# A six-layer decoder on one core: the first cross layer's keys, statistics and query rows in space of their own, and single buffers in the first softmax

## The chip, the core and the metric

The kernel runs on one core of a Trainium2 chip. The core has five engines that each run their own queue of instructions in order and meet through semaphores: TensorE (PE, matrix products), VectorE (DVE), ScalarE (ACT), GpSimd (POOL) and SyncE (SP), which here only issues DMAs. The metric is the time of one execution on the device in microseconds; lower is better.

## What is computed

The reference is a decoder of six sublayers over `x` of shape (64, 128, 256) (64 batches of 128 positions, 256 features), all in float32. Each sublayer normalises its input and adds its result to `x`:

```python
x = x + _L0_attn_ref(_layernorm(x), ...)                      # A: attention in a window of 7
x = x + _L0_xattn_ref(_layernorm(x), ctx, ctx, mask, Wp, bp)  # B: masked attention over ctx
x = x + _L0_ffn_ref(_layernorm(x), ...)                       # C: slots
x = x + _L1_attn_ref(_layernorm(x), ...)                      # D: causal attention with a learned bias
x = x + _L1_xattn_ref(_layernorm(x), ctx, ...)                # E: attention over ctx
x = x + _L1_ffn_ref(_layernorm(x), ...)                       # F: quantised weights, convolution
```

Two of them matter here. The first layer, A, softmaxes the scores of each query against 7 neighbouring keys and weighs them with a learned profile `conn` before it normalises again:

```python
attn = softmax(einsum('bhld,bhlwd->bhlw', Q, Kw) / sqrt(DH))
fw = attn * conn
fw = fw / (fw.sum(axis=-1, keepdims=True) + 1e-09)
out = einsum('bhlw,bhlwd->bhld', fw, Vw)
```

The first cross layer, B, has no projections of queries, keys and values: its queries are the normalised rows of `x`, its keys and values the rows of `ctx`, in 16 heads of 16. A score whose query or key is masked is replaced by -1e9, and the weights are multiplied by that mask again.

## The kernel before

**Groups and stages.** The 64 batches are cut into 16 groups of four (`GB`). The layers run one after the other in stages: `stage_window` (A), `stage_cross0` (B, with the slot layer C run inside it by `tick`), `stage_attn` twice (D and E) and `stage_bitnet` (F). Between stages `x` goes through DRAM: `Flow` (L62) loads a group by one DMA of 512 KB on SP's queue (L80, into one of eight buffers) and stores a finished group (L90).

**Layer A.** The generator `window_project` does a group's layer norm statistics and its q, k and v. `ln_stats` (L122) issues per group four pairs `bn_stats`, `bn_aggr` (L141, L142) and an addition (L143) on DVE, and a power (L144) on POOL that gives one over the standard deviation. `row_bias` (L262) is the small DVE operation behind it. The projections are L166 on PE. `window_products` (L320) multiplies shifted keys and queries on POOL, `window_scores` (L332) sums them on PE. `window_softmax` is called once a group: the maximum L348, the difference L350, the exponential on ACT L351, the product with `conn` L353, two sums L356 and L357, the combined sum L358, a reciprocal L359, and the weights `fw` L361. It takes its tiles `m`, `e`, `ec`, `se`, `scn`, `fw` from the pool `wa`, which holds two buffers for each. `window_values` spreads `fw` over the positions on PE (L372), multiplies it with the shifted values into `pv` (L378) and sums to `oT` (L382) on DVE; `window_out` multiplies by the output weights (L175, PE) and adds to `x` (L392, DVE). In its loop the stage staggers these steps over several groups. At the last step of a group, from the second on, it also runs one entry of the list `later`, which prepares a later layer: `prep_b` (for B), `prep_c`, `prep_f`, `prep_d`, and then six steps of `prep_fire`, which builds the bias table of D.

**Layer B's preparation.** `prep_cross0` (L752) loads the output weights, their bias and the mask, builds in `head_rows` the small masks `par`, `row` and `one`, and writes the mask rows (0 or -1e9) to the DRAM tile `mrow`.

**Layer B itself.** `stage_cross0` (L652) begins by filling two key buffers `kt0` and `kt1` (128x4x512, float32, 8 KB in each partition) with the columns of `one`: four copies each on POOL (L661). Four value tiles `va` are cleared and given a column of ones (L665, L666), the first context group is loaded (L645) and the first `x` group. `load_keys(0)` then issues 16 DMAs on SP for the keys of group 0: eight of 64 KB from `ctxT` (L679) and eight mask rows from `mrow` (L680). `prep(bi)` is called per batch. On the first batch of a group it loads the next group, calls `ln_stats`, makes `r4` (L695) and the row bias `nm` (L262). For every batch ACT makes the query rows `qp` (L704) and fills `va` (L708). `more` transposes `qp` on PE (L717) and writes the queries `qt` on ACT (L721). `attention_stage` (L579) clears two `negmax` tiles on POOL, and runs two half steps per batch: PE scores in bursts (L490), a maximum on DVE (L517), its transposition into the queries (L529, L531), the shifted scores and their exponential on ACT (L513), the weighing of the values (L543), the division (L555) and the output.

**What sets the order.** Each engine's queue is written out when the program is built. The tile framework places an instruction in its engine's queue where its operands and its buffer allow, which can be ahead of instructions that stand earlier in the Python text, and it sets the semaphores. A tile in a pool can't be written before the earlier user of the same space has finished, so where a pool is opened decides how early its first instruction can stand. In the kernel before, the pools of `stage_cross0` (`wb`, `wb1`, `wb3`, `wc2`) are opened after those of `stage_window` (`wa`, `wa1`) are closed, and lie on the same space. DMAs of SP go out in the order of its queue. The functions of the change, as they stand before:

Of the kernel before, what the change touches and what calls it, by code (L numbers as in the profile page):

```python
# [16 lines left out]
D = 256  # L17
H = 16
DH = 16
S = 128  # L20
# [319 lines left out]
def window_softmax(k, w, t, wp, w1):  # L340
    nc = k.nc
    sv = t.scp[:, 0 : WIN * 64].rearrange("p (w l) -> p l w", l=64)

    def over(x):
        return x.unsqueeze(2).to_broadcast([128, 64, WIN])

    m = wp.tile([128, 64], F, tag="m", name="m")
    nc.vector.tensor_reduce(m, sv, AX.X, ALU.max)  # L348
    e = wp.tile([128, 64, WIN], F, tag="e", name="e")
    nc.vector.tensor_tensor(e, sv, over(m), ALU.subtract)  # L350
    nc.scalar.activation(e, e, AF.Exp)  # L351
    ec = wp.tile([128, 64, WIN], F, tag="ec", name="ec")
    nc.vector.tensor_tensor(ec, e, w.conn.unsqueeze(1).to_broadcast([128, 64, WIN]), ALU.mult)  # L353
    se = wp.tile([128, 64], F, tag="se", name="se")
    sc = wp.tile([128, 64], F, tag="scn", name="scn")
    nc.vector.tensor_reduce(se, e, AX.X, ALU.add)  # L356
    nc.vector.tensor_reduce(sc, ec, AX.X, ALU.add)  # L357
    nc.vector.scalar_tensor_tensor(se, se, 1e-9, sc, ALU.mult, ALU.add)  # L358
    nc.vector.reciprocal(se, se)  # L359
    t.fw = wp.tile([128, 64, WIN], F, tag="fw", name="fw")  # L360
    nc.vector.tensor_tensor(t.fw, ec, over(se), ALU.mult)  # L361
# [289 lines left out]
def stage_cross0(k, w, wc):  # L651
# [3 lines left out]
    with k.tc.tile_pool(name="wb", bufs=2) as wp, k.tc.tile_pool(name="wb1", bufs=1) as w1, \  # L655
            k.tc.tile_pool(name="wb3", bufs=3) as w3, k.tc.tile_pool(name="wc2", bufs=2) as c2:
        kts, vas = [], []
        for i in range(2):
            kt = w1.tile([128, 4, GB * S], F, name=f"kt{i}")
            for c in range(4):  # L660
                nc.gpsimd.tensor_copy(kt[:, c], w.one[:, c : c + 1].to_broadcast([128, GB * S]))  # L661
            kts.append(kt)
        for i in range(4):
# [7 lines left out]

        def load_keys(g):


            kt = kts[g % 2]
            for par in range(2):
                for r in range(4):
                    rows = slice(32 * r + 16 * par, 32 * r + 16 * par + 16)
                    nc.sync.dma_start(out=kt[rows, par::2, :], in_=k.a["ctxT"][g, rows])  # L679
                    nc.sync.dma_start(  # L680
                        out=kt[32 * r + 20 - 16 * par : 32 * r + 21 - 16 * par, par::2, :],
                        in_=w.mrow[g : g + 1].unsqueeze(1).to_broadcast([1, 2, GB * S]),
                    )

        load_keys(0)

        def prep(bi):
            g, b = divmod(bi, GB)
            if b == 0:
                k.flow.reach(g + 1)  # L690
                if g + 1 < k.G:
                    cxs[g + 1] = load_group(k, wp, g + 1, 3)
                mv, rs = ln_stats(k, wp, g)
                r4 = wp.tile([S, GB], F, tag="r4", name="r4")
                nc.vector.tensor_scalar(r4, rs, 0.25, None, ALU.mult)  # L695
                stats[g] = r4, row_bias(k, wp, mv, r4)
            r4, nm = stats[g]
# [4 lines left out]
            xb = k.x[g][:, b, :]  # L702
            qp = wp.tile([S, D], F, tag="qp", name="qp")
            nc.scalar.activation(  # L704
# [46 lines left out]

def prep_cross0(k, pool):  # L752
    nc = k.nc
    w = Ctx()
    w.wp = load(k, pool, "b_wp")
    w.bp = load_row(k, pool, "b_bp")
    w.mask = load(k, pool, "mask")
    w.mask2 = pool.tile([S, k.NB], F, name="mask2")
    nc.vector.tensor_tensor(w.mask2, w.mask, w.mask, ALU.mult)
    w.par = pool.tile([128, 2], F, name="b_par")  # L760
    w.row = pool.tile([128, 2], F, name="b_row")
    w.one = pool.tile([128, 4], F, name="b_one")
    head_rows(k, w.par, w.row, w.one)

    w.mrow = k.dram.tile([k.G, GB * S], F, name="mrow")
    with k.tc.tile_pool(name="maskw", bufs=1) as cp:
        mr = load(k, cp, "maskr")
        nc.vector.tensor_scalar(mr, mr, 0.0, -1.0e9, ALU.is_equal, ALU.mult)
        nc.sync.dma_start(out=w.mrow, in_=mr)
    return w  # L770

# [286 lines left out]
def prep_fire(k, pool):  # L1058
# [4 lines left out]
    with k.tc.tile_pool(name="firew", bufs=1) as cp:  # L1063
# [21 lines left out]

        bm = cp.tile([S, 4, 4, S], F, name="bm")
        nc.scalar.copy(bm, b2.rearrange("p (c r) -> p r c", r=4).unsqueeze(3).to_broadcast([S, 4, 4, S]))
        bmf = bm.rearrange("p r c l -> p (r c) l")
        nc.gpsimd.affine_select(bmf, bmf, [[0, 16], [1, S]], ALU.is_ge, NEG, 0, -1)
        yield  # L1090
# [13 lines left out]
        for half in range(2):  # L1104
# [8 lines left out]
            for q in range(2):  # L1113
                pv = ps[:, q].rearrange("p (t c r) -> p r c t", c=4, r=4)
                own = slice(64 * half + 32 * q, 64 * half + 32 * q + 32)
                for r in range(4):
                    nc.vector.tensor_tensor(bt[:, r, :, own], pv[:, r], bm[:, r, :, own], ALU.add)
            yield
# [384 lines left out]
def decoder(tc, a):  # L1503
# [8 lines left out]
    with ExitStack() as ctx:  # L1512
# [10 lines left out]
        with tc.tile_pool(name="w1", bufs=1) as w1:  # L1523
            with tc.tile_pool(name="w0", bufs=1) as w0:
                with tc.tile_pool(name="wA", bufs=1) as wA:
# [3 lines left out]
                    def prep_b():  # L1529
                        p.b = prep_cross0(k, w0)  # L1530

# [142 lines left out]
```

## Time and profile before

| | |
|---|---|
| time, median of 3 runs | 3145.78 us (3145.59 to 3149.34) |
| time of the profiled execution | 3156.87 us |
| its span in the trace | 3155.1 us |
| mean granted clock of TensorE | 0.92 |
| busy: PE, of it weight loads beside | 2773.7 us (88%), PEld 1784.5 us (57%) |
| busy: DVE | 2343.6 us (74%) |
| busy: ACT | 1600.3 us (51%) |
| busy: POOL | 453.4 us (14%) |
| layer A ends (last L392) | 570.3 us |
| layer B's first maximum (L517) begins | 586.73 us |

Every time within the kernel is counted from the start of the span of one profiled execution. The engines' busy times overlap, so they don't add up to the span. A row of the timeline has the start, the busy time of the group, the engine and line, the operation with its output and inputs, the number of instructions, and in brackets how long the engine had been idle and what released it. The row "L490 ... sm<-kt,qt" is thus the score matmul of line 490 with output `sm`. The profile's page counts for the whole span 256 maxima L517 of 1221 ns, 128 products L320 of 1995 ns and 64 powers L144 of 1059 ns into `ln_rs`, the form that A, B and some later stages share.

### The profile page before, as it was taken

How to read it: one execution, taken by the hardware profiler on the slowest of the kernel's cores; microseconds unless marked ns; L12 is line 12 of the kernel's file. 1: busy time of each engine (PE TensorE's matmuls, PEld its weight loads, DVE VectorE, ACT ScalarE, POOL GpSimd, SP SyncE). 2: the span in 40 equal slices, each digit the busy share in tenths (PEclk: the TensorE clock that was granted, in tenths of full speed). 3: DMA queues.
4: the chain of work that ended last, by engine and by line, in shares of the span. 5: the costliest groups of instructions: out<-in, count | busy, mean ns of one | idle time of the engine just before them, and what ended most of it. 6: DMA issues, size and time to landing. Idle time of an engine off the chain costs nothing.

```text
span 3155.1 us, 63533 instructions
## 1 busy us (share of the span) xinstructions
PE 2773.7 (88%) x26850; PEld 1784.5 (57%) x26876; DVE 2343.6 (74%) x4533; ACT 1600.3 (51%) x2684; POOL 453.4 (14%) x358
## 2 busy tenths in 40 slices
PE   5889988689989899889999999979999998888887
PEld 2334533466666677546666666656666665334343
DVE  7898788757777777568888888845455546898897
ACT  3132221366656566445555555455555556766663
POOL 7565663100000000010000000020000000100000
PEclk9888888789999899889999999989999999999898
DMA  4110101201111111100000000011111101011000
GB/s 152 42 39 29 41 27 40 76 29 38 53 56 42 46 32 35 41 29 15 28 28 28 28 28 28 28 48 42 42 54 48 42 29 41 14 40 34 27 21 27
DMA packets 60012, 123.83 MB, mean 39 GB/s; under 512 B 9088, under 2 KB 34064, under 8 KB 59472
## 3 DMA queue, kind: packets, MB, share of 16 engines
q1 hardware_dynamic: 59168, 118.28, 10.9%
q8 instruction: 213, 3.49, 0.4%
q0 software_dynamic: 560, 1.49, 0.2%
q14 instruction: 71, 0.58, 0.1%
HBM read 77.76 MB, written 41.98 MB: 38 GB/s over the span
## 4 chain that ended last, share of the span: by engine, by line
PE 50%; DVE 35%; ACT 8%; POOL 3%; DMA 2%; issue 2%; SPq 0%; POOLq 0%; DVEq 0%; ACTq 0%
PE ps L175 9%; PE ps L166 8%; PE sm L490 8%; PE ps L543 4%; PE se L490 4%; DVE negmax L517 3%; PE ps L1189 3%; PE cv L1370 3%; DVE sb L504 3%; DVE e L510 3%; DVE hs L1424 2%; DVE pv L378 2%; DVE hp L1360 2%; DVE oT L382 2%; PE ps L555 2%
## 5 line engine op out<-in xcount | busy, mean ns | idle before, releaser
L490 PE MATMUL sm<-kt,qt 32*128 32x128 f32 x6144 | 537.0, 297 | 68.1 <-DVE negmax L517 39.7
L490 PEld LDWEIGHTS sm<-kt,qt 32*128 32x128 f32 x6144 | 434.8, 192 | 239.4 <-DVE negmax L517 72.3
L490 PE MATMUL se<-q,kt 32*128 32x128 f32 x6144 | 481.0, 292 | 55.3 <-DVE e L510 26.2
L517 DVE TENSOR_REDUCE negmax<-sm 128x8 f32<-128x1024 f32 x256 | 312.6, 1221 | 238.2 <-PE se L490 232.0
L490 PEld LDWEIGHTS se<-q,kt 32*128 32x128 f32 x6144 | 402.5, 193 | 82.8 <-issue 36.9
L513 ACT ACTIVATE e<-se 128x1024 f32<-128x1024 f32 x256 | 261.4, 1021 | 168.1 <-PE se L490 160.1
L1370 PE MATMUL cv<-hp,taps 128*128 128x512 f32 x480 | 247.9, 654 | 35.6 <-DVE hp L1360 35.3
L320 POOL TENSOR_TENSOR pr<-pad,qt 128x896 f32<-128x896 f32 x128 | 252.5, 1995 | 168.3 <-PE s L332 128.3
L548 ACT COPY avs<-ps 128x512 f32<-128x512 f32 x192 | 112.2, 584 | 192.1 <-PE ps L543 192.1
L504 DVE TENSOR_TENSOR sb<-sm,bias_s 128x1024 f32<-128x1024 f32 x128 | 156.0, 1219 | 63.4 <-PE se L490 60.2
L511 ACT ACTIVATE e<-e 128x1024 f32<-128x1024 f32 x128 | 135.3, 1057 | 123.6 <-DVE e L510 123.3
L1370 PEld LDWEIGHTS cv<-hp,taps 128*128 128x128 f32 x480 | 95.5, 209 | 143.8 <-issue 86.5
L378 DVE TENSOR_TENSOR pv<-sc,pad 128x896 f32<-128x896 f32 x128 | 139.1, 1093 | 43.7 <-PE sc L372 43.7
L144 POOL TENSOR_TENSOR ln<-ln,expo 128x4 f32<-128x4 f32 x32 | 32.3, 1008 | 960.7 <-DVE ln L143 708.6
L144 POOL TENSOR_TENSOR ln_rs<-ln_ve,expo 128x4 f32<-128x4 f32 x64 | 67.7, 1059 | 652.3 <-DVE ln_ve L143 451.9
L510 DVE TENSOR_TENSOR e<-se,bias_t 128x1024 f32<-128x1024 f32 x128 | 155.6, 1215 | 2.4 <-ACT e L511 1.3
L517 DVE TENSOR_REDUCE negmax<-sb 128x8 f32<-128x1024 f32 x128 | 154.8, 1209 | 0.0
L382 DVE TENSOR_REDUCE oT<-pv 128x128 f32<-128x896 f32 x128 | 139.2, 1093 | 1.2
L372 PE MATMUL sc<-fw,spread 32*128 32x448 f32 x512 | 105.3, 664 | 33.6 <-DVE pv L378 28.9
L531 DVE TENSOR_TENSOR q<-ps,qt 128x512 f32<-128x512 f32 x192 | 130.9, 682 | 1.6 <-PE ps L529 1.6
L555 PE MATMUL ps<-ident,avs 128*128 128x128 f32 x768 | 119.2, 279 | 0.8 <-ACT avs L548 0.8
L141 DVE BATCH_NORM_STATS2 ln_st<-x 128x6 f32<-128x256 f32 x256 | 99.3, 426 | 10.6 <-DMA x<-ab 9.4
(338 smaller groups left out, 5819.9 us busy)
## 6 DMA issues: line engine op xcount, KB each, us to landing
x<-in_x_dram SPq DMA_DIRECT2D x16, 512.0 KB
ab<-x SPq DMA_DIRECT2D x16, 512.0 KB
x<-ab SPq DMA_DIRECT2D x16, 512.0 KB
cx<-in_ctx_dram SPq DMA_DIRECT2D x16, 512.0 KB
kt<-in_ctxT_dram SPq DMA_DIRECT2D x128, 64.0 KB
cd<-x SPq DMA_DIRECT2D x16, 512.0 KB
x<-cd SPq DMA_DIRECT2D x16, 512.0 KB
de<-x SPq DMA_DIRECT2D x16, 512.0 KB
```

The costliest lines, as they stand in the source:

```text
L166: k.nc.tensor.matmul(out, w[:, kc, c0 : c0 + cn], rhsT[:, kc, n0 : n0 + n], start=(kc == 0), stop=(kc == 1),)
L175: k.nc.tensor.matmul(out, aT[:, kc, :], w[:, kc, :], start=(kc == 0), stop=(kc == 1))
L320: k.nc.gpsimd.tensor_tensor(pr[:, c], shift_windows(t.kt, b, c), t.qt[:, c, b, :].unsqueeze(1).to_broadcast([128, WIN, S]), ALU.mult,)
L378: nc.vector.tensor_tensor(pv, bc[th][:, :, 0 : WIN * 64].rearrange("p c (l w) -> p c l w", w=WIN), shift_windows2(t.vt, b, th), ALU.mult,)
L382: nc.vector.tensor_reduce(oT[:, :, 64 * th : 64 * th + 64], pv, AX.X, ALU.add)
L490: k.nc.tensor.matmul(ts[side][:, rr, c * S : (c + 1) * S], st[rows, c, :], mv[rows, c, :], start=True, stop=True,)
L504: nc.vector.tensor_tensor(sb, src, bias_s[:, hf * 2 : hf * 2 + 2, :], ALU.add)
L510: nc.vector.tensor_tensor(e, est, bias_t[:, hf * 2 : hf * 2 + 2, :], ALU.add)
L513: nc.scalar.activation(e, est, AF.Exp)
L517: nc.vector.tensor_reduce(b.lay.extra(b.nm, hf * 2), src.rearrange("p r (c m) -> p r c m", m=S), AX.X, ALU.max, negate=True,)
L555: nc.tensor.transpose(tv[:, c * S : (c + 1) * S], b.avs[:, c, :], k.ident)
L1370: nc.tensor.matmul(pc, w.taps[:, CONV_PE.index(j), t, :], hp[:, :, t : t + S], start=(t == 0), stop=(t == 2),)
```

## The change

Three things are moved, and the arithmetic stays the same.

1. In `window_softmax` all tiles but `fw` come from the pool `wa1`, which has one buffer for each instead of two.
2. A new pool `wbe` with two buffers is opened around `stage_window` and `stage_cross0`, beside `w0`. The statistics tiles, `r4`, `nm` and the query rows `qp` of layer B come from it. `kt0` comes from `w0` now, so neither lies on space of the window stage. Filling `kt0`, and `load_keys(0)`, with its 16 DMAs, are called at the end of `prep_cross0`, that is in the window stage's loop; `kt1` is still filled at the head of `stage_cross0`.
3. `prep_fire` has no temporary `bm` any more: the causal part of the bias table is written straight into `bias_t` and added to in place.

```diff
 def window_softmax(k, w, t, wp, w1):
-    m = wp.tile([128, 64], F, tag="m", name="m")
+    m = w1.tile([128, 64], F, tag="m", name="m")
...
-    e = wp.tile([128, 64, WIN], F, tag="e", name="e")
+    e = w1.tile([128, 64, WIN], F, tag="e", name="e")
...
-    ec = wp.tile([128, 64, WIN], F, tag="ec", name="ec")
+    ec = w1.tile([128, 64, WIN], F, tag="ec", name="ec")
...
-    se = wp.tile([128, 64], F, tag="se", name="se")
-    sc = wp.tile([128, 64], F, tag="scn", name="scn")
+    se = w1.tile([128, 64], F, tag="se", name="se")
+    sc = w1.tile([128, 64], F, tag="scn", name="scn")
...
 def stage_cross0(k, w, wc):
-        kts, vas = [], []
-        for i in range(2):
-            kt = w1.tile([128, 4, GB * S], F, name=f"kt{i}")
-            for c in range(4):
-                nc.gpsimd.tensor_copy(kt[:, c], w.one[:, c : c + 1].to_broadcast([128, GB * S]))
-            kts.append(kt)
+        kts, vas, early, load_keys = w.kts, w.vas, w.early, w.load_keys
+        w.make_keys(w1)
...
-        load_keys(0)
-
         def prep(bi):
...
-                mv, rs = ln_stats(k, wp, g)
-                r4 = wp.tile([S, GB], F, tag="r4", name="r4")
+                mv, rs = ln_stats(k, early, g)
+                r4 = early.tile([S, GB], F, tag="r4", name="r4")
                 nc.vector.tensor_scalar(r4, rs, 0.25, None, ALU.mult)
-                stats[g] = r4, row_bias(k, wp, mv, r4)
+                stats[g] = r4, row_bias(k, early, mv, r4)
...
-            qp = wp.tile([S, D], F, tag="qp", name="qp")
+            qp = early.tile([S, D], F, tag="qp", name="qp")
...
-def prep_cross0(k, pool):
+def prep_cross0(k, pool, early):
...
+    w.kts, w.vas = [], []
+
+    def make_keys(pool):
+        kt = pool.tile([128, 4, GB * S], F, name=f"kt{len(w.kts)}")
+        for c in range(4):
+            nc.gpsimd.tensor_copy(kt[:, c], w.one[:, c : c + 1].to_broadcast([128, GB * S]))
+        w.kts.append(kt)
+
+    w.make_keys = make_keys
+    make_keys(pool)
...
+    load_keys(0)
     return w
...
-        bm = cp.tile([S, 4, 4, S], F, name="bm")
-        nc.scalar.copy(bm, b2.rearrange("p (c r) -> p r c", r=4).unsqueeze(3).to_broadcast([S, 4, 4, S]))
-        bmf = bm.rearrange("p r c l -> p (r c) l")
-        nc.gpsimd.affine_select(bmf, bmf, [[0, 16], [1, S]], ALU.is_ge, NEG, 0, -1)
+        nc.scalar.copy(bt, b2.rearrange("p (c r) -> p r c", r=4).unsqueeze(3).to_broadcast([S, 4, 4, S]))
+        btf = bt.rearrange("p r c l -> p (r c) l")
+        nc.gpsimd.affine_select(btf, btf, [[0, 16], [1, S]], ALU.is_ge, NEG, 0, -1)
...
-                    nc.vector.tensor_tensor(bt[:, r, :, own], pv[:, r], bm[:, r, :, own], ALU.add)
+                    nc.vector.tensor_tensor(bt[:, r, :, own], pv[:, r], bt[:, r, :, own], ALU.add)
...
-            with tc.tile_pool(name="w0", bufs=1) as w0:
+            with tc.tile_pool(name="w0", bufs=1) as w0, tc.tile_pool(name="wbe", bufs=2) as wbe:
...
-                        p.b = prep_cross0(k, w0)
+                        p.b = prep_cross0(k, w0, wbe)
```

The body of `load_keys` moves along unchanged.

Set side by side, the two kernels' queues read as follows. PE's order is the same. On SP the store of `mrow` and the 16 loads of `kt0` now stand ahead of the load of `x` of group 4. On POOL four of the eight key copies stand near the start, and the powers L144 of the cross layer's groups 0 to 3 stand in the window stage. On DVE the statistics of the cross layer's groups 0 to 3 stand there too; the statistics of the window stage's groups 5 to 7 and some small rows of D, E and C (`bqs`, `bks`, `bvb`, `c_hs`) have moved from ahead of the first softmax to behind it. On ACT the first two query rows `qp` stand in the window stage. Behind the hand-over from A to B nothing differs.

More of the change, by code (lines that the diff above doesn't have):

```diff
@@ L670, in stage_cross0 @@
         stats = {}
[L672 to L683, printed above, removed]
-        load_keys(0)
         def prep(bi):
@@ L749, in head_rows @@
         k.nc.vector.tensor_reduce(one[:, c : c + 1], rows[:, 1 - c % 2, c], AX.X, ALU.add)
-def prep_cross0(k, pool):
+def prep_cross0(k, pool, early):
     nc = k.nc
     w = Ctx()
+    w.early = early
     w.wp = load(k, pool, "b_wp")
@@ L769, in prep_cross0, with load_keys @@
         nc.sync.dma_start(out=w.mrow, in_=mr)
+    w.kts, w.vas = [], []
[6 more added lines that the diff above has]
+    make_keys(pool)
+    def load_keys(g):
+        kt = w.kts[g % 2]
+        for par in range(2):
+            for r in range(4):
+                rows = slice(32 * r + 16 * par, 32 * r + 16 * par + 16)
+                nc.sync.dma_start(out=kt[rows, par::2, :], in_=k.a["ctxT"][g, rows])
+                nc.sync.dma_start(
+                    out=kt[32 * r + 20 - 16 * par : 32 * r + 21 - 16 * par, par::2, :],
+                    in_=w.mrow[g : g + 1].unsqueeze(1).to_broadcast([1, 2, GB * S]),
+                )
+    w.load_keys = load_keys
+    load_keys(0)
     return w
```

## The prediction

> **What bounds the kernel now.** I read the profile's page first: its chain that ended last is half TensorE (PE 50%) and a third VectorE (DVE 35%), and the change touches only the first 600 of 3155 us: the first layer (to 570 us), its start and the hand-over to the first cross layer. The table of 20 us windows shows no engine full there (0 to 600 us: PE 498, DVE 494, ACT 146, POOL 338 us busy), so engines wait for one another, and what counts is which wait ends last. The chain of waits and the timelines show it in three places.
>
> The hand-over, in the timeline of all engines:
>
> ```profile
> 569.93 0.42 DVE L392 TENSOR_TENSOR x<-ps,x 128x256 f32<-128x256 f32 x1 [1.84 <-PE ps L175]
> 570.04 4.50 POOL L661 COPY kt<-b_one 128x512 f32<-128x512 f32 x8 [3.91 <-PE ps L175]
> ...
> 576.87 2.00 POOL L144 TENSOR_TENSOR ln_rs<-ln_ve,expo 128x4 f32<-128x4 f32 x2
> ...
> 579.50 1.09 ACT L704 ACTIVATE qp<-x,ln_nm,r 128x256 f32<-128x256 f32 x2 [2.47 <-DVE ln_nm L262]
> ...
> 581.54 2.19 PE L490 MATMUL sm<-kt,qt 32*128 32x128 f32 x16 [0.21 <-issue]
> ...
> 586.73 1.21 DVE L517 TENSOR_REDUCE negmax<-sm 128x8 f32<-128x1024 f32 x1
> ...
> 588.00 2.15 PE L490 MATMUL sm<-kt,qt 32*128 32x128 f32 x16 [4.27 <-DVE negmax L517]
> ```
>
> The first layer ends at 570.3; then a serial chain runs: 8 key copies, 8 memsets and the power L144 on POOL, statistics, query rows, scores. The first maximum waits 3 us more, because DVE still does statistics of other groups. It ends at 587.9.
>
> The steady first layer: one softmax (L348) per group of four batches cuts it into blocks. Starts 235.34, 262.17, 289.06 give 26.8 and 26.9 us; starts 393.90, 424.20, 454.71, 485.32, 513.63, 539.18 give 30.3, 30.5, 30.6, 28.3, 25.6. The slow ones hold no layer norm statistics (L141); the quick ones do. DVE, then PE, first a quick block, then a slow one:
>
> ```profile
> 268.26 0.22 DVE L358 SCALAR_TENSOR_TENSOR se<-se,scn 128x64 f32<-128x64 f32 x1
> 271.79 1.98 DVE L361 TENSOR_TENSOR fw<-ec,se 128x448 f32<-128x448 f32 x1
> ...
> 429.03 1.46 DVE L358 SCALAR_TENSOR_TENSOR se<-se,scn 128x64 f32<-128x64 f32 x1
> 433.80 2.01 DVE L361 TENSOR_TENSOR fw<-ec,se 128x448 f32<-128x448 f32 x1
> ```
>
> ```profile
> 272.85 2.08 PE L175 MATMUL ps<-t_a_wo,oT 128*128 128x256 f32 x4
> 274.72 2.15 PE L166 MATMUL ps<-xnT,t_a_wq 128*128 128x512 f32 x4
> ...
> 436.95 2.05 PE L175 MATMUL ps<-t_a_wo,oT 128*128 128x256 f32 x4 [1.06 <-DVE oT L382]
> 438.79 3.62 PE L166 MATMUL ps<-xnT,t_a_wq 128*128 128x512 f32 x4
> ```
>
> In the slow block L358 stands right behind the sums and meets a POOL product (L320, 428.45 to 432.3): 1.46 instead of 0.22 us. Then fw (2.01 against 0.61 where POOL is idle) stands ahead of the oT for which PE waits. From L350 to PE's L175 it is 10.8 us against 8.8, and PE restarts slow: its eight L166 take 5.2 against 3.65. That is 2.0 + 1.6 of the 3.6 us.
>
> The start, DVE, then SP and PE:
>
> ```profile
> 53.63 1.92 DVE L262 SCALAR_TENSOR_TENSOR ln_nm<-ln_mv,ln_rs 128x4 f32<-128x4 f32 x1 [4.99 <-POOL ln_rs L144]
> ...
> 61.82 0.61 DVE L348 TENSOR_REDUCE m<-s 128x64 f32<-128x448 f32 x1
> ```
>
> ```profile
> 13.78 0.42 SPq L80 DMA_DIRECT2D x<-in_x_dram  x1
> ```
>
> ```profile
> 63.24 1.72 PE L332 MATMUL s<-pr,gather 128*32 128x448 f32 x8 [6.47 <-DVE e L350]
> ```
>
> The first softmax could start when PE has its scores (53.1), but DVE is held until 61.82 by small work queued ahead, slowed by POOL; PE idles 6.5 us for it.
>
> **The change part by part.** On PE the order of instructions is the same in both kernels; the others differ only up to the hand-over.
>
> *Hand-over.* Four of eight kt copies, the first two query rows, both groups' statistics and kt0's 16 loads are gone from it. What is left: L392 ends 570.3; transposes L717 0.7 (580.15 to 580.87), qt 0.7 (to 581.54), scores 2.2: 573.9. POOL: four copies 2.25 from 570.04, and negmax is cleared 2.2 after the copies (574.48 to 576.69): 574.5. This is late next, and sets it. Maximum 1.2: 575.7 against 587.9, **-12.2**. The bounds: -9.2 if DVE still keeps the maximum waiting 3 us, -12.8 if the memset isn't waited for. kt1's 16 loads now take kt0's place on SP (571.8 to 582.4); they end 6.5 us behind the second burst's start instead of 4.6. The ninth burst needs them, 24 us behind it (negmax at 614.5), so they stay hidden. The context load (570.03) and va are needed only by L543, 13 us on.
>
> *Blocks.* Statistics of cross groups 0 to 3 now stand in the blocks from 393.90, 424.20, 454.71 and 485.32, three more L141 in the next, five in the last. DVE's order becomes that of the quick blocks word for word: L358 behind a pv, fw behind the oT. I take 26.9 for each. Savings: 3.4 + 3.6 + 3.7 + 1.4 = 12.1. In the first, r4 waits for POOL's L144, a new wait: 279.2 in the quick block's clock, +1.0 power, +0.3 small, two qp 1.1 and two L727 0.9 until pv may start, 282.0 against 279.6; behind it pv has 1.8 of slack (its next wait on PE), so 0.6 is lost. ACT's queue holds a pad copy behind qp for 3 us; POOL's product needs it, but waits for PE there anyway (2.2). The end, where DVE is full (19.96 of 20 us): +1.0 for three L141 and -0.6 for the wait they fill, -1.2 for L358, +1.7 for five: +0.9. Sum **-10.6**. Between 0, if the new work keeps the slow form (2.0 us of statistics in 6.1 us of waits per block), and -12.1. I take the quick blocks' value, since the order is the same and POOL's L320 starts 2.4 us behind L350 in both.
>
> The slow PE restart has a row (3.62 against 2.15 for four L166). The Trainium skill, "TensorE: Matmul & The Clock Gate", "What's actually happening", has PE's clock halve after an idle window and come back only after some 3.4 us of sustained work. [...]
>
> *Start.* kt0 is filled at 8 to 10 us, where POOL idles 13.4 us (2.3 of it used). kt0's 16 loads and mrow go ahead of x of group 4 on SP, which is in order. mrow waits for DVE (19.98, unchanged), so x of group 4 goes from 13.78 to about 20.3 + 14 x 0.6 + 0.4 = 29, and the loads behind it move by some 9 us. They lie beside: x of group 4 is needed for the power L144 at 52.6. DVE, having the statistics of groups 5 to 7 and the d and e rows behind the first softmax now, starts that at about 57.2 (L144 one product later, 55.3, then L262 1.9): -4.6. The moved work is 5.9 us of statistics, 3.9 of bvb and 1.3 to 7.8 of small rows (free of POOL or not); it meets waits of DVE of 6.95 (before 76.43), 2.85 (before 92.83) and 2.7 (to 105.6). Followed by hand, ec of the second softmax comes 3.5 earlier. I take **-3.5**, between -4.6 (all hidden) and +8 (12.6 not hidden).
>
> *Nothing:* single buffers of the softmax (one use per 26 us, DVE in order; ACT's exp 0.58 long done), and bias_t built in place (same instructions). If e were still read, L350 would wait 0.6 at most.
>
> **Sum.** -12.2 - 10.6 - 3.5 = -26.3 us against the profiled execution: 3156.87 - 26.3 = 3130.6. That execution (span 3155.1) is 11.1 us above the median of the runs, 3145.78; the same loss there gives **3119.5**. What 2570 us behind the hand-over do with a shifted phase I leave at 0, +-4.
>
> **Rivals.**
> 1. The blocks don't get quick (a port phase, not the order, made them so): the middle is 0 and the total -15.7: 3130. For it: fw still takes 2.0 in the quick blocks. Against: four quick blocks with statistics, four slow without. 0.20.
> 2. The start loses, +8 instead of -3.5: 3131. For it: POOL is busy 20.0 of 20 us at 40 to 60, and each small DVE row can wait 1.9. Against: the waits named. 0.10.
> 3. Slower: x of group 4 comes late on SP. DVE is in order, so its statistics hold the first softmax, and with it the whole layer. It costs what the landing exceeds 57 us; from 28 us behind the issue it bites, from 51 us (22.8 + 28) it outweighs the rest: 3152 for 57 us. The longest landing on the chain there is 9.05 (t_c_wo). 0.04.
> 4. It doesn't do what it says, or 1 and 2 together: 3142. Against: the order has the query rows ahead of the hand-over. 0.06.
>
> **How the numbers follow.** The forecast, 3119.5, has 0.60 (3111 to 3127 by its bounds). Range: below, all hidden (-4.6 -12.1 -12.8 = -29.5) and -4 behind: 3112, and some for PE warm: 3108; above, rivals 1 and 2 with +6: 3137. Faster by over 0.2% (6.3 us, about what a measurement of this kernel can tell from no change): 0.60 + 0.20 + 0.10 = 0.90; within: 0.06; slower: 0.04.
>
> **What would show it.** In the changed kernel: the first L517 ends 5.4 us behind the last L392, not 17.6; L348 to L348 of 27 in blocks 10 to 13; L358 at 0.2 there; the first L348 near 57; x of group 4 issued near 29. The prediction is wrong if blocks stay at 30, if DVE waits for DMA before 60 us, or if stages behind 600 us change by more than 4 us.

## The result, and the profile after

The changed kernel takes 3132.77 us (median of 7 runs, 3129.92 to 3143.02) against 3147.40 us for the kernel before (7 runs, 3144.88 to 3150.20): ratio 0.9958, 95% interval 0.9944 to 0.9972, so 13 us faster (9 to 18). The forecast was 26.3 us. Its profiled execution took 3137.45 us, span 3135.7.

The time is read in five pieces, cut at rows of DVE: the softmax (L348) of the fifth group, that of the tenth, the last L392 of layer A (its end for the third piece, its start for the fourth, which overlap by its 0.42 us), and the first maximum L517 of layer B. The column "again" is a second profile of the same kernel (run "again" below).

| piece | before | after | again | change | forecast |
|---|---|---|---|---|---|
| start to fifth L348 | 209.84 | 213.79 | 214.03 | +4.0, +4.2 | -3.5 |
| fifth to tenth L348 (bias table) | 157.11 | 157.22 | 152.81 | +0.1, -4.3 | 0 |
| tenth L348 to end of last L392 | 203.40 | 198.48 | 198.24 | -4.9, -5.2 | -10.6 |
| last L392 to first L517 | 16.80 | 4.51 | 4.49 | -12.3, -12.3 | -12.2 |
| behind it | 2568.4 | 2562.1 | 2566.1 | -6.2, -2.3 | 0 |

The first L517 comes 13.15 us earlier in after (586.73 to 573.58) and 17.6 in again. What lies behind it has the same queues and varies by itself: the last piece has 2556 to 2566 us in the seven profiles here with the changed kernel's queues, and 2563 to 2568 in the three with those of before (before, single_only, order_only); whether the change takes part in that is not shown. The bias table's piece varies too: its last interval took 38.73 us in after and 33.88 in shift, whose queues are the same.

**The hand-over**, in the timeline of all engines of the changed kernel:

```profile
569.07 0.42 DVE L392 TENSOR_TENSOR x<-ps,x 128x256 f32<-128x256 f32 x1 [1.84 <-PE ps L175]
569.10 2.28 POOL L758 COPY kt<-b_one 128x512 f32<-128x512 f32 x4 [3.83 <-PE ps L175]
...
569.55 1.12 PE L698 MATMUL ps<-ident,qp 128*128 128x128 f32 x4 [0.52 <-DVE x L392]
...
571.31 2.11 PE L490 MATMUL sm<-kt,qt 32*128 32x128 f32 x16 [0.64 <-ACT qt L702]
...
573.54 0.21 POOL L591 MEMSET negmax<- 128x144 f32 x1
573.58 1.22 DVE L517 TENSOR_REDUCE negmax<-sm 128x8 f32<-128x1024 f32 x1
```

The transposes start behind the last L392, the scores end at 573.42, and the clearing of the first of two negmax tiles at 573.54 (the row shows the second); then the maximum starts. This is the forecast chain, link by link, though its two last links lie only 0.1 us apart; the maximum ends 5.3 us behind the last L392 (forecast 5.4). The 2.11 us of L490 show PE at the slow rate: the granted clock is 0.50 from 570 to 590 us.

**The start**, DVE, then POOL, first a row of before, then after. L348 comes at 62.73 (before 61.82, forecast 57.2):

```profile
19.41 0.21 DVE L759 TENSOR_TENSOR mask<-t_mask 128x64 f32<-128x64 f32 x1
...
21.61 0.23 DVE L742 TENSOR_TENSOR mask<-t_mask 128x64 f32<-128x64 f32 x1 [2.47 <-DMA t_mask<-in_mask_dram]
...
57.18 5.63 DVE L262 SCALAR_TENSOR_TENSOR ln_nm<-ln_mv,ln_rs 128x4 f32<-128x4 f32 x1 [16.55 <-POOL ln_rs L144]
62.73 0.61 DVE L348 TENSOR_REDUCE m<-s 128x64 f32<-128x448 f32 x1
```

```profile
35.16 15.17 POOL L320 TENSOR_TENSOR pr<-pad,qt 128x896 f32<-128x896 f32 x8
...
52.59 1.01 POOL L144 TENSOR_TENSOR ln_rs<-ln_ve,expo 128x4 f32<-128x4 f32 x1
...
36.78 15.16 POOL L320 TENSOR_TENSOR pr<-pad,qt 128x896 f32<-128x896 f32 x8
...
54.19 1.98 POOL L320 TENSOR_TENSOR pr<-pad,qt 128x896 f32<-128x896 f32 x1
56.10 1.04 POOL L144 TENSOR_TENSOR ln_rs<-ln_ve,expo 128x4 f32<-128x4 f32 x1
57.10 5.69 POOL L320 TENSOR_TENSOR pr<-pad,qt 128x896 f32<-128x896 f32 x3
```

L144 stands one product later than before, as forecast, but ends at 57.1 and not at 55.3, because all of POOL's products start 1.6 us later (36.78 instead of 35.16). That goes back to DVE: it waits 2.47 us for the load of `t_mask` ahead of the first statistics, where it did not wait before. All ten profiles with kt0 filled early on POOL have this wait (1.2 to 3.5 us), the four without have none. Why the load lands later isn't shown; one thing that the early copies push back is a DMA that POOL issues (`t_c_b`, 10.31 instead of 8.04). Then the small L262 lasts as long as three products of POOL; it was reckoned at one (1.9). The second block takes 30.17 us instead of 25.70: the statistics of groups 5 to 7 and C's, D's and E's rows stand between its products.

**The blocks** from the tenth L348 on take 27.02, 27.64, **33.69**, 25.92, 26.89 and 24.40 us (before: 26.95, 30.30, 30.51, 30.61, 28.31, 25.55). All but one are within 0.8 us of the forecast or below it. The slow one, DVE, then PE, then POOL:

```profile
429.17 0.75 DVE L141 BATCH_NORM_STATS2 ln_st<-x 128x6 f32<-128x256 f32 x2 [1.02 <-DMA x<-ab]
...
429.92 2.33 DVE L353 TENSOR_TENSOR ec<-e,conn 128x448 f32<-128x448 f32 x1
...
434.62 2.13 DVE L358 SCALAR_TENSOR_TENSOR se<-se,scn 128x64 f32<-128x64 f32 x1
```

```profile
434.75 1.02 PE L372 MATMUL sc<-fw,spread 32*128 32x448 f32 x4 [3.19 <-DVE pv L378]
438.80 1.86 PE L372 MATMUL sc<-fw,spread 32*128 32x448 f32 x4 [3.02 <-DVE pv L378]
```

```profile
429.80 4.26 POOL L320 TENSOR_TENSOR pr<-pad,qt 128x896 f32<-128x896 f32 x2 [2.56 <-PE s L332]
434.33 2.34 POOL L286 TENSOR_TENSOR x<-x,t_a_bo 128x1024 f32<-128x1024 f32 x1 [0.27 <-ACT xn L271]
```

The moved statistics wait for a DMA: the reload of `x` for the cross layer's group 1. The wait is short (1.02), but DVE comes out of it just behind POOL's product (L353 2.33 instead of 0.62) and later behind L286 (L358 2.13 instead of 0.21). PE waits 6.2 us and restarts slow. Why the reload is late shows on SP (the store of a group and the reload into its buffer; the reload waits for the store) and in the DMA engines' busy tenths (40 slices of 0.15 us, from 421.0 us):

```profile
421.72 0.32 SPq L90 DMA_DIRECT2D ab<-x  x1
425.89 0.32 SPq L80 DMA_DIRECT2D x<-ab  x1
```

```profile
DMA  0000000005899999897001000000000000000009
...
q8 instruction: 1, 0.02, 1.4%
```

The store of 512 KB and its reload lie 4.17 us apart here, 2.61 in the next block (453.50 and 456.11). In this window a packet of the instruction queue q8 stands as well; the trace's packet records have it at 16 KB and 1.34 us, beginning with the store, and the store's packets spread over 2.89 us instead of 1.43.

### The profile page after: what moved, and what is told of

Same layout as the page of the kernel before. It is cut to its first block, busy times and chain, and to the rows that moved or that the text cites. A ratio compares the mean times of both kernels' runs of the same rounds, so it can differ in the third digit from the quotient of the medians.

```text
span 3135.7 us, 63532 instructions
## 1 busy us (share of the span) xinstructions
PE 2764.9 (88%) x26850; PEld 1778.6 (57%) x26876; DVE 2333.9 (74%) x4533; ACT 1601.1 (51%) x2684; POOL 454.9 (15%) x358
## 3 DMA queue, kind: packets, MB, share of 16 engines
q0 software_dynamic: 560, 1.49, 0.2%
## 4 chain that ended last, share of the span: by engine, by line
PE 49%; DVE 35%; ACT 8%; POOL 3%; DMA 2%; issue 2%; SPq 0%; POOLq 0%; DVEq 0%; ACTq 0%
PE ps L175 9%; PE sm L490 8%; PE ps L166 7%; PE ps L543 4%; PE se L490 4%; DVE negmax L517 3%; PE ps L1197 3%; DVE sb L504 3%; DVE e L510 3%; PE cv L1378 3%; DVE hs L1432 2%; DVE pv L378 2%; DVE hp L1368 2%; DVE oT L382 2%; PE ps L555 2%
## 5 line engine op out<-in xcount | busy, mean ns | idle before, releaser
L490 PE MATMUL sm<-kt,qt 32*128 32x128 f32 x6144 | 539.5, 298 | 67.9 <-DVE negmax L517 39.7
L490 PEld LDWEIGHTS sm<-kt,qt 32*128 32x128 f32 x6144 | 436.9, 193 | 239.2 <-DVE negmax L517 70.3
L490 PE MATMUL se<-q,kt 32*128 32x128 f32 x6144 | 481.8, 292 | 54.7 <-DVE e L510 26.3
L517 DVE TENSOR_REDUCE negmax<-sm 128x8 f32<-128x1024 f32 x256 | 312.6, 1221 | 235.6 <-PE se L490 232.1
L490 PEld LDWEIGHTS se<-q,kt 32*128 32x128 f32 x6144 | 403.3, 193 | 82.5 <-issue 36.7
L144 POOL TENSOR_TENSOR ln<-ln,expo 128x4 f32<-128x4 f32 x32 | 32.3, 1009 | 957.1 <-DVE ln L143 669.0
L144 POOL TENSOR_TENSOR ln_rs<-ln_ve,expo 128x4 f32<-128x4 f32 x64 | 67.8, 1059 | 650.4 <-DVE ln_ve L143 450.6
L517 DVE TENSOR_REDUCE negmax<-sb 128x8 f32<-128x1024 f32 x128 | 154.8, 1209 | 0.0
L141 DVE BATCH_NORM_STATS2 ln_st<-x 128x6 f32<-128x256 f32 x256 | 98.5, 400 | 12.5 <-DMA x<-ab 11.3
```

Source lines behind the costliest of these rows:

```text
L490: k.nc.tensor.matmul(ts[side][:, rr, c * S : (c + 1) * S], st[rows, c, :], mv[rows, c, :], start=True, stop=True,)
L517: nc.vector.tensor_reduce(b.lay.extra(b.nm, hf * 2), src.rearrange("p r (c m) -> p r c m", m=S), AX.X, ALU.max, negate=True,)
```

## The experiments

All ratios are to the kernel before on the same chip. The columns are the pieces above.

| run | ratio (95%) | fifth L348 | tenth L348 to last L392 | to first L517 |
|---|---|---|---|---|
| before | 1 | 209.84 | 203.40 | 16.80 |
| after | 0.9958 (0.9944 to 0.9972) | 213.79 | 198.48 | 4.51 |
| again | 0.9942 (0.9922 to 0.9962) | 214.03 | 198.24 | 4.49 |
| single_only | 0.9989 (0.9977 to 1.0002) | 208.46 | 205.63 | 16.73 |
| keys_only | 0.9989 (0.9975 to 1.0003) | 212.05 | 204.62 | 12.27 |
| stats_only | 0.9945 (0.9925 to 0.9964) | 209.28 | 197.93 | 12.80 |
| order_only | 0.9952 (0.9930 to 0.9973) | 208.47 | 189.59 | 16.80 |
| hold_stats | 0.9945 (0.9926 to 0.9964) | 214.81 | 196.76 | 4.50 |
| shift | 0.9940 (0.9918 to 0.9962) | 214.51 | 194.81 | 4.51 |
| late_keys | 0.9924 (0.9907 to 0.9941) | 206.68 | 194.91 | 4.50 |
| late_again | 0.9919 (0.9902 to 0.9935) | 206.67 | 197.19 | 4.51 |
| late_hold | 0.9933 (0.9911 to 0.9954) | 207.13 | 194.45 | 4.50 |
| keys_order | 0.9920 (0.9903 to 0.9937) | 206.56 | 189.85 | 12.29 |
| two_held | 0.9919 (0.9899 to 0.9939) | 207.97 | 196.12 | 4.51 |

Kernels with the start's queues of before (before, single_only, order_only) differ by 1.4 us at the fifth L348, so differences below that are not read. In the piece from the tenth L348, before and single_only have the same queues and differ by 2.2; after, again, shift, late_keys and late_again have the same queues there and spread over 194.8 to 198.5.

**again: is the slow block chance?** No edit.

> The changed kernel once more, for a second profile. Its first profile lost 4.0 us at the start (L348 of group 4 at 213.79 instead of 209.84) and won only 4.9 in the blocks behind, because one block (425.67 to 459.36) took 33.7 us: there DVE waited 1.0 us for the reload of x from the store between the layers (L141), its next products met POOL's, and PE waited 6.2 us. If that block is the rule (the added statistics wait for the reload each time), this profile has it again at 32 to 34 us. If it is the chance of one slow store, all blocks from the tenth on take 26 to 28 us here, the first layer ends near 563 us instead of 569.5, and the spread of the times (3129.9 to 3143.0) is such chances. The 5.6 us that L262 took behind three products of POOL should come again under both, since the queues fix it. Time: 13 to 15 us below before.

The block took 32.38 us, the store and reload lay 4.36 us apart, L141 waited 1.11, L262 took 5.62. So neither is chance. By the medians the kernel was 18.2 us below before, more than the 13 to 15 expected. stats_only has the block at 32.08, late_keys at 29.06, shift at 28.96, late_again at 30.52, and the queues of this stretch are the same in all of them. The waits for the reload don't tell them apart (0.67 to 1.49 us); what does is which of two rows comes first. In shift, DVE, then POOL:

```profile
425.90 0.59 DVE L353 TENSOR_TENSOR ec<-e,conn 128x448 f32<-128x448 f32 x1
```

```profile
426.00 4.23 POOL L320 TENSOR_TENSOR pr<-pad,qt 128x896 f32<-128x896 f32 x2 [2.56 <-PE s L332]
```

Here L353 starts 0.1 us ahead of the product and takes 0.59; in after it started 0.12 behind it and took 2.33. It starts 0.12 to 0.58 us behind the product in after, again and stats_only (blocks of 32.1 to 33.7), and with it or ahead of it in shift, late_keys and late_again (29.0 to 30.5).

**late_keys: SP's order and the start.**

```diff
 def prep_cross0(k, pool, early):
-    load_keys(0)
...
-    stage_window(k, wa, [prep_b, prep_c, prep_f, prep_d] + [prep_bias] * 6)
+    stage_window(k, wa, [prep_b, prep_c, prep_f, prep_d] + [prep_bias] * 6 + [lambda: p.b.load_keys(0)])
```

> The changed kernel with the 16 loads of kt0 called at the end of the window stage's list of preparations, so that on SP they stand behind x of group 7 instead of ahead of x of group 4. Theory (the start): the loads ahead of x of group 4 reordered DVE and POOL at the start and cost 4.0 us up to group 4. Then this kernel has L348 of group 4 at 209 to 210 us, the first L348 at or before 61.8, and is 3 to 5 us faster than the changed kernel. Rival (the start's loss has nothing to do with SP; it comes from the copies into kt0 on POOL or from the early statistics): the start stays at 213 to 214 and the time within 1.5 us of the changed kernel. Under both the hand-over keeps its gain: first L517 4 to 5.5 us behind the last L392.

The rival falls, and the start wins more than the theory had: it comes out below before. DVE, then SP of late_keys:

```profile
54.63 1.91 DVE L262 SCALAR_TENSOR_TENSOR ln_nm<-ln_mv,ln_rs 128x4 f32<-128x4 f32 x1 [5.00 <-POOL ln_rs L144]
```

```profile
14.88 0.50 SPq L80 DMA_DIRECT2D x<-in_x_dram  x1
...
37.60 0.72 SPq L771 DMA_DIRECT2D kt<-in_ctxT_dram  x1
```

`x` of group 4 goes at 14.88 again; DVE has the window statistics ahead of the softmax, L144 stands where it did, and the rows of E, whose loads now come behind the keys, stand behind the first softmax. The fifth L348 comes 7.4 us earlier than in again, and the median on that chip is 3123.97 against 3131.61. The edit moves one call, but the orders of DVE and POOL change with it, so it shows that the place of the loads costs the start its time, not which of the queues carries it. DVE still waits 1.20 us for `t_mask` here.

**stats_only and keys_only: the two halves of the early set-up.**

```diff
 # stats_only: kt0 at the head of the cross stage, as before
-    make_keys(pool)
-    load_keys(0)
...
+        w.make_keys(w1)
         w.make_keys(w1)
...
+        load_keys(0)
 # keys_only: statistics and query rows from the cross stage's pool
-                mv, rs = ln_stats(k, early, g)
+                mv, rs = ln_stats(k, wp, g)
...
-            qp = early.tile([S, D], F, tag="qp", name="qp")
+            qp = wp.tile([S, D], F, tag="qp", name="qp")
```

> The changed kernel with kt0 filled and loaded at the head of the cross stage again, as before; only the statistics and query rows have space of their own (and the softmax single buffers). Theory: the start is that of before (first L348 at 61 to 62, group 4 at 209 to 211), the blocks from the tenth on are those of the changed kernel (26 to 28 us, but for a block held by the reload), and at the hand-over the loads of kt0 (12 of 16 are needed by the first burst, 1.27 us a pair on SP) hold the first scores until some 11 us behind the last L392: the first L517 comes 13 to 14 us behind it instead of 17.6. Sum -8 to -14 us against before. Rival (the blocks gain nothing from the statistics): the first layer ends at 570 as before, sum 0 to -4.

> The changed kernel with statistics, r4, nm and qp of the cross layer from the pool of the cross stage again; only kt0 is filled and loaded early. Theory: the start loses as in the changed kernel (+3 to +5 us at group 4), the blocks from the tenth on stay slow (30.3 to 30.6 three times), and the hand-over wins 2 to 5 us, since the serial chain of statistics, power, query rows and transposes stays but starts 2.2 us earlier on POOL. Sum -2 to +3 us against before. Rival (the blocks are made quick by the shifted phase, not by the statistics in them): blocks of 27 us here too and a sum of -8 or lower.

stats_only alone wins 4.0 us at the hand-over, keys_only 4.5, both together 12.3: either chain, the keys or the statistics, holds the first maximum by itself. In stats_only it is the loads of kt0 on SP that hold the scores:

```profile
574.20 1.61 PE L490 MATMUL sm<-kt,qt 32*128 32x128 f32 x10 [0.41 <-DMA kt<-mrow]
```

The blocks are quick with the statistics (197.9) and not without (204.6); the start loses with the early loads only (212.05 against 209.28). keys_only can't be told from before; its blocks (30.65, 29.90, 28.41, 29.79) are slow, if not the 30.3 to 30.6 expected. stats_only, 17.7 us below before where 8 to 14 were expected, can't be told from the changed kernel in again: as they are called in the change, the early keys lose at the start (4.5 us) half of what they win at the hand-over (8.3).

**single_only: the single buffers.** The edit is the change's first part (all tiles of `window_softmax` but `fw` from `wa1`).

> The kernel before with only the single buffers in the softmax (m, e, ec, se and scn), nothing else. The prediction costs this at nothing: each tile is used once in 26 us. Expected: within 2 us of before (ratio 0.9995 to 1.0005), start and blocks as before (first L348 at 61 to 62, blocks of 30 to 31 us), hand-over 16.8 us. If the space that it frees or a wait for a buffer matters, the first softmaxes or the blocks show it.

Start and hand-over are those of before, and so are the first three of the slow blocks (30.42, 30.57, 30.64); the next two (29.21, 26.71) are 0.9 and 1.2 us longer, with the same queues. The ratio's interval takes in 1. Nothing is seen in the time, as forecast, to within some 0.2%.

**order_only: what makes a block quick.** Theory: the place of L358 behind a pv; rival: the statistics in the waits, or the phase. `issue_after(i)` puts what is built in its block behind instruction i in that engine's queue.

```diff
+    with k.tc.issue_after(k.first.ins):     # window groups 10 to 15; first: the last pv built with th == 0
         nc.vector.scalar_tensor_tensor(se, se, 1e-9, sc, ALU.mult, ALU.add)
```

> The kernel before with one thing changed: in the softmaxes of the window stage's last six groups, L358 is queued behind the next pv (L378) instead of right behind the two sums, so L361 stands behind an oT; no early statistics, no early keys. Theory of the prediction (the order makes a block quick): the blocks of 30.3, 30.5, 30.6 and 28.3 us become 26 to 27.5, and the time falls by 8 to 12 us. Rival (the statistics that fill DVE's wait, or the phase, make it quick): they stay at 29.5 to 30.6, time -3 to +1 us.

The blocks became 26.96, 26.34, 26.83, 26.87, 26.90 and 24.39 us with no statistics in them, 13.8 us less to the last L392, and the kernel 0.5% faster (14.1 us by the medians, 8 to 12 expected). DVE, then PE (lines shifted: L360 was L358, L365 the fw of L361):

```profile
419.15 1.08 DVE L382 TENSOR_TENSOR pv<-sc,pad 128x896 f32<-128x896 f32 x1
420.14 0.59 DVE L360 SCALAR_TENSOR_TENSOR se<-se,scn 128x64 f32<-128x64 f32 x1
...
424.05 2.01 DVE L365 TENSOR_TENSOR fw<-ec,se 128x448 f32<-128x448 f32 x1
```

```profile
425.38 1.98 PE L175 MATMUL ps<-t_a_wo,oT 128*128 128x256 f32 x4
427.20 1.88 PE L166 MATMUL ps<-xnT,t_a_wq 128*128 128x512 f32 x4
```

fw still takes 2.01 us, but the oT that PE needs is ahead of it, and L166 runs warm. Rival 1 of the prediction falls: the order makes the blocks quick. It also shows that the statistics are a burden there and no filling: with them the piece takes 194 to 198 us, without 189.6.

**hold_stats: the wait for the reload.** Theory: the wait at its place costs 5 us or more.

```diff
-                mv, rs = ln_stats(k, early, g)
+                if g == 1:
+                    with k.tc.issue_after(k.sums[10 + g].ins):   # L357 of window group 11
+                        mv, rs = ln_stats(k, early, g)
+                else:
+                    mv, rs = ln_stats(k, early, g)
```

> The changed kernel with one move on DVE: the first two statistics of the cross layer's group 1 stand at the end of their block (behind the third L382 before L143) instead of ahead of L353; every other queue is the same. In the changed kernel's two profiles this is the block of 33.7 and 32.4 us: L141 waits 1.0 to 1.1 us for the reload of x, whose store ends late (4.2 to 4.4 us from issue to the reload's issue, 2.6 in the other blocks), because an instruction fetch shares its DMA engine. Theory: the wait makes L353 and L358 meet POOL's products (2.3 and 2.1 us) and PE wait 6.2 us; without the wait at this place the block takes 26.9 to 28 us and the kernel is 4 to 6 us faster than the changed kernel (-18 to -21 against before). The late store itself stays. Rival (the block is slow because DVE comes out of the block before it late, not because of the wait): 31 to 33 us again, time within 1.5 us of the changed kernel.

The block takes 28.52, just above the 26.9 to 28 expected, but the next takes 30.02: the two took 59.6 (after) and 59.3 (again), and take 58.5. Nor was the store late in this profile (the reload went 2.78 us behind it), so the reload would hardly have held the old place either. In hold_stats, DVE:

```profile
442.21 1.91 DVE L680 TENSOR_SCALAR r<-ln_rs 128x4 f32<-128x4 f32 x1 [1.13 <-POOL ln_rs L144]
```

The statistics, now at the block's end, push L144 back; `r4` (L680) waits for it, meets a product (1.91), and PE goes cold (its eight L166 take 4.49 instead of 3.60). That second bill is again a collision and no rule: late_hold below has the same queues here, its L680 took 0.17, and its next block 26.94. So without the wait the block takes 28.5 to 28.6: 3.9 and 5.1 us less than in again and after, but only 0.4 less than the 29.0 where L353 came first, and 1.6 more than the 26.9 of the forecast. The time can't be told from that of again; the 4 to 6 us that the theory gave aren't seen.

**late_hold: both repairs.** The edits of late_keys and hold_stats.

> Both repairs together: kt0's loads behind x of group 7 on SP, and the first two statistics of the cross layer's group 1 at the end of their block. In the kernel with the late loads alone that block took 29.06 us (its L353 met no product, 0.59 us, but its L358 did, 1.45). Theory: the block takes 26.9 to 27.6 us, 1.5 to 2 us less, and the rest stays: -25 to -27 us against before. Rival: as the late loads alone, -23 to -25.

Here the store is late (4.54 us to the reload) and DVE doesn't wait for it. The block took 28.60 instead of 29.06: the rival is the nearer one. The time, 19.4 us below before by the medians, meets neither range and is not lower than with the late loads alone.

**shift: the 5.6 us of L262.** One unused tile ahead of the pads.

```diff
+        gap = wp.tile([128, 24], F, name="gap")
+        nc.gpsimd.memset(gap, 0.0)
         pads = []
```

> The changed kernel with one more tile of 96 bytes per partition in the pool of the window stage, cleared once on POOL, so that the tiles behind it lie elsewhere; the queues stay the same otherwise. It is for the L262 ahead of the first softmax, which took 5.6 us, as long as three products of POOL, in three profiles of kernels with both early parts, and 1.9, as long as one, with kt0 early alone, whose queues are the same there. If the place of the tiles decides, L262 takes 1.9 here and the first L348 starts near 59; if it is how the two instructions start against each other in these queues, it takes 5.6 again and L348 starts at 62 to 64.

L262 took 5.63 again, so the place of the tiles doesn't decide. keys_only has the same queues there and 1.9. DVE, then POOL of keys_only:

```profile
57.66 1.91 DVE L262 SCALAR_TENSOR_TENSOR ln_nm<-ln_mv,ln_rs 128x4 f32<-128x4 f32 x1 [18.40 <-POOL ln_rs L144]
```

```profile
57.59 8.05 POOL L320 TENSOR_TENSOR pr<-pad,qt 128x896 f32<-128x896 f32 x4
```

What lets L262 in behind one product here and behind three there stays open.

**keys_order, two_held and late_again: is there a better version?** keys_order is late_keys with order_only's edit and the statistics at the hand-over. two_held is late_hold with that edit, where only groups 0 and 1 have early statistics:

```diff
+                if g < 2:
+                    with k.tc.issue_after(k.sums[12 + g].ins):
+                        mv, rs = ln_stats(k, early, g)
+                    with k.tc.issue_after(k.sums[13 + g].ins):
+                        r4 = early.tile([S, GB], F, tag="r4", name="r4")
...
+                else:
+                    with k.tc.issue_after(k.negs[-8].ins):       # the eighth L517 back
+                        mv, rs = ln_stats(k, wp, g)
```

> kt0 early, its loads behind x of group 7 on SP, and L358 queued behind a pv in the last six groups; statistics and query rows at the hand-over as before. Theory: the last L392 comes 189 to 191 us behind the tenth L348, as with the order alone, start as with the late loads (group 4 at 206 to 208), gap to the first L517 12.3 us as with kt0 alone: 20 to 24 us below before. If the statistics in the blocks were needed for the quick form, the window stage would take 195 us or more here.

> What the runs point to, put together: kt0's loads behind x of group 7 on SP; L358 queued behind a pv in the window stage's last six groups; only the cross layer's groups 0 and 1 have their statistics early, in the blocks of window groups 12 and 13 behind the sums (their reload has long landed there), their r4 and nm a block later; the statistics of the groups behind them are queued behind the eighth maximum back, so that none stands ahead of the first maxima. Theory: start as with the late loads (group 4 at 206 to 208), blocks of 26 to 27.5 without a wait for a reload, last L392 some 191 to 194 us behind the tenth L348 (189.6 with the order alone, 198.2 in the changed kernel), first L517 4 to 5 us behind the last L392. Sum 28 to 33 us below before, 3 to 8 below the late loads alone. Rival (the statistics cost DVE the same wherever they stand, in the cross stage as in the window stage): what the window stage wins the cross stage gives back, time as with the late loads alone, within 2 us.

> The changed kernel with kt0's loads behind x of group 7, once more, to stand beside the others on one chip and for a second profile: start at 206 to 208 for group 4, the block held by the reload 28 to 33 us, 20 to 25 us below before.

All three end alike (0.9919 to 0.9920). keys_order keeps the quick blocks (189.85) and pays 7.8 us more at the hand-over; two_held pays in its last two blocks, which got `r4` and the second statistics (30.16 and 27.65 instead of 26.90 and 24.39), most of what it wins at the hand-over. The expectation for two_held, 28 to 33 us below before and 3 to 8 below the late loads alone, stands at its edge by the medians (28.1 and 3.0) and isn't met by the ratios, which are equal; the rival can't be excluded. All three are some 25 us (0.8%) below before. The late loads are also below the same kernel with the loads early, in each of three pairs measured together: 7.6 us (late_keys and again), 2.8 (late_hold and hold_stats) and 5.8 (late_again and shift, which differ by shift's unused tile too); moving one call is enough for it.

## Why the prediction was wrong

The direction and the three places were right; two of the three sizes were not.

- **Hand-over, -12.2: right** (-12.3), with the link named as the last one, the clearing of negmax, by 0.1 us. The scores took the 2.2 us that the sum has for them (L490 2.11).
- **Blocks, -10.6: the mechanism was right, the size too large** (-4.9 and -5.2, half of it; -6.2 to -8.6 in shift, late_keys and late_again, with the same queues there). The failed step is "I take 26.9 for each". Three of the four slow blocks came within 0.8 us of it or below (27.64, 25.92, 26.89), and the end, the last block and what is behind it, took 0.6 more than before (forecast 0.9). One took 33.69, 6.8 more. The working followed one new wait in the blocks, that of r4 for L144, and left out another that the moved L141 brings along: its input is a reload that waits for a store, and it stands only 8 us behind the L392 that frees the buffer (421.23 to 429.17). What that wait costs hangs on whether L353 comes out of it ahead of POOL's product or behind it: the block takes 29.0 to 33.7 us with the wait, and 28.5 to 28.6 without it. The rest, up to 1.7 us there, comes with the statistics themselves: order_only shows what the blocks take without any, 189.6 us, so the four groups' statistics cost 5 to 9 us in this piece.
- **Start, -3.5: the sign was wrong** (+4.0, +4.2). Three terms failed. "mrow waits for DVE (19.98, unchanged)": it went at 22.36, because DVE waited 2.47 us for `t_mask` (a wait for a DMA before 60 us is one of the prediction's own signs), and so L144, one product later as forecast, ended at 57.1 instead of 55.3 (+1.8). "then L262 1.9": 5.63 (+3.7, in four profiles of four with early statistics and the key loads ahead of `x` of group 4; why stays open). And the moved work "meets waits of DVE": the second block took 4.5 us more, 1.7 of it won back in the third. late_keys shows that the place of the key loads is the cause: with the loads behind `x` of group 7 L262 takes 1.91, the second block 26.51, and the fifth L348 comes 3.2 us earlier than before.
- **Nothing for the single buffers: right** within 0.2% (single_only).
- **PE's slow restart** stands in the prediction's rows right behind a hole of 1.06 us (L166 3.62 against 2.15). The granted clock of before was down ahead of the hole: 1.00 from 435.0 to 435.6 us, 0.50 from 435.7, while the hole lasts from 435.9 to 436.95, and 1.00 again from 442.5. The quick block has it at 0.50 too, from 271.9 to 275.2. So both blocks restart slow, the slow one for 6.7 us instead of 3.3; that the hole starts it isn't shown. The few us that the range's low end has for a warm PE appear in no run: at the hand-over the granted clock is 0.50 in before (580 to 600 us) and in after (570 to 590).
- Rival 2 (the start loses, 3131) is close to the measured median by its time, but with only half of its +8; the blocks made the other half. `x` of group 4, the slower rival, went at 31.70 (forecast 29) and held nothing.
- The range's low end (3108) counted on everything hidden; its high end, 3137, was right, and 3132.77 lies in it. With the start at +4.1, the blocks at -5.0 and the hand-over at -12.3, the forecast's own sum gives -13.2, the measured ratio's 13. That they agree so well is partly luck: the sum leaves out the pieces that vary by themselves (+0.1 and -6.2 us in after, -4.3 and -2.3 in again), and again's ratio gives 18. By the sign "if stages behind 600 us change by more than 4 us" one profile of two fails (-6.2), but profiles with the same queues differ by as much.

## What to carry to other kernels

When work is hoisted into waits, list the inputs of every hoisted instruction with the DMA that brings each and what that DMA waits for; here a wait of about 1 us for such a DMA went with a block 0.4 to 5 us longer, depending on which of two engines came first behind it, so one profile doesn't price it. Where a transfer that can go at any time is called decides what a scheduler puts behind it: moving 16 loads behind the first layer's own cost one line and won 3 to 8 us. And if a change seems to make a stage quick through the order that it happens to produce, impose that order by itself: it won more in its piece alone (13.8 us) than with the work that brought it (4.9 to 8.6 with the same queues).

## What the runs showed of the hardware

A store of 512 KB took 1.43 us by its packets alone and 2.5 to 3.5 us where a 16 KB instruction packet (0.96 to 1.65 us) began with it or lay in it (after, again, shift, late_keys, late_again, late_hold, stats_only), and the reload that waits for it went 1.2 to 2.2 us later. In the seven other profiles no such packet overlapped the store, and it took 1.43 to 1.62; in the kernel before, the packet began 0.56 us behind it. The Trainium skill, "DMA: Bandwidth & Descriptors", "Queues, rings and completion order", has each DMA engine take turns between its queues by whole packets. The trace agrees in six of the seven, where the store grew by one such packet within 0.2 us (in after by 1.46, with a packet of 1.34); in stats_only it grew by 2.05 with a packet of 0.96.

A 128x4 operation on DVE (L262) beside POOL's products lasted as long as one of them (1.9 us) in most profiles, and as three (5.63, 5.62, 5.62, 5.63) in four. The Trainium skill, "SBUF — State Buffer", "SBUF: two separate sides", has the port that the two share held for one whole instruction. The 1.9 us agree with that; the 5.6 us don't follow from it.
